# Two sequences' slots for the first routed pairs, three for the last twelve

## The chip, the cores and the metric

One core of a Trainium2 chip runs the kernel, a forward pass of two layers in float32. The metric is device time in microseconds for one execution. TensorE is called PE, VectorE DVE, ScalarE ACT, GpSimd POOL and SyncE SP, as the profile does.

## The reference

Four sequences of 512 tokens with 256 features go through two layers. The first layer is an attention inside each token, then two experts of which each token takes one. The second is a selective scan along the sequence with eight states, then a mixture of 64 routed experts (six per token) and one shared expert. What matters here is the mixture: each expert takes only the first 64 tokens that choose it, in the order of the tokens of all four sequences, and the rest is dropped.

```python
x = x + _L0_attn_ref(_layernorm(x), ...)     # B, L, E, H = (4, 512, 256, 16)
x = x + _L0_ffn_ref(_layernorm(x), ...)      # 2 experts, FF = 1024, one per token
x = x + _L1_attn_ref(_layernorm(x), ...)     # scan, d_state = 8:
    _, h = associative_scan(combine, (dA, dBu), axis=1)
    y = jnp.einsum('bldn,bln->bld', h, C_ssm) + x * D_param
x = x + _L1_ffn_ref(_layernorm(x), ...)      # H, F, E, TOP_K, CAP = 256, 176, 64, 6, 64:
    topk_w, topk_idx = jax.lax.top_k(softmax(x @ gate_w.T), TOP_K)
    pos = jnp.arange(T * TOP_K) - starts[eid_s]        # place within the expert
    valid = pos < CAP
    g = silu(einsum('ech,ehf->ecf', buf, w_gate)); u = einsum('ech,ehf->ecf', buf, w_up)
    d = jnp.einsum('ecf,efh->ech', g * u, w_down)
    y = jnp.einsum('tkh,tk->th', out_exp.reshape(T, TOP_K, H), topk_w)
    y = y + silu(x @ sh_gate.T) * (x @ sh_up.T) @ sh_down.T
```

## The kernel before

Steps are Python closures that record instructions; `_together` deals several lists of them into one order by their lengths, and a scheduler then sets the order on each engine. At run time every engine works its own queue strictly in that order and waits on semaphores.

The first layer's experts are taken in tiles of 128 tokens (`hidden`, `turned`, `down`), two halves to a tile, and run beside the scans of the first three sequences. `down` ends with a scatter of `yo` into `back` by POOL, and `join` loads `back` on SP and adds it to the sequence's `x`.

The second layer of a sequence is `scan_inputs` (layernorm, projections, softplus), eight times `state`, `scan_out`, `scores`, `choose` and `ranked`. In `state`, PE spreads one row of B and one of C over the partitions (`bc`), DVE multiplies, scans twice and multiplies again, and ACT computes the decays. The products are added up by an accumulating DMA of POOL for the first three sequences and on DVE for the fourth. `scores` also stores the normalized rows with their 64 scores in DRAM (`xrow`). `choose` marks each token's six experts, `ranked` takes the first 64 tokens of each expert by eight rounds of a maximum of eight and a replacement, and `slots` merges such lists of several sequences into the 64 places of each expert, and into the row numbers that gathers and scatters use.

The routed experts go in 32 pairs (`routed`). For a pair, POOL gathers 128 rows (`gather`, tile `xg`), PE turns them (`tokens`, `mtp`) and multiplies by gate and up (`up`, `mgu`), PE turns the result (`turn`, `mth`), multiplies by the down weights (`down`, `mpo`), ACT and DVE scale the halves (`mdw`), and POOL scatters them, adding, into one of two tables `ytab`. The 1.03 MB of a pair's weights are loaded on SP (`moe_weights`), six pairs ahead: pair 0's buffer is in a pool of its own, the other five lie where the first layer's weights were.

`slots(0)` merges the lists of three sequences and comes after the third scan, so no pair starts before that. The steps of `shared` of the first two sequences come there as well. Then the 32 pairs are dealt among the fourth sequence's scan and the third's shared expert; the fourth's shared expert comes after the pairs. The tables are loaded and added to three sequences at the end. If an expert still has room after three sequences and the fourth wants it, the block behind `tc.If(any_new > 0)` computes all pairs again for the fourth sequence.

Of the kernel before, what the change touches and what calls it, by code (L numbers as in the profile page):

```python
# [16 lines left out]
P = 128  # L17
# [20 lines left out]
AHEAD = 1  # L38
AHEAD0 = 5
PART = NB - 1  # L40
TP = PART * L
TL = T - TP
# [16 lines left out]
def two_layer_kernel(  # L59
# [30 lines left out]
    moew = ctx.enter_context(tc.tile_pool(name="moew", bufs=AHEAD))  # L90
# [5 lines left out]
    xrow = dram.tile([TP, XR], F32, name="xrow")  # L96
    xlast = dram.tile([TL, XR], F32, name="xlast")
# [87 lines left out]
    lists = keep.tile([64, 4, CAP], F32, name="lists")  # L185
    later_lists = keep.tile([64, 3, CAP], F32, name="later_lists")
    masks = keep.tile([P, NJ, 2, E1], F32, name="masks")
    raws = [keep.tile([P, E1 // 2], F32, name=f"raw{i}") for i in range(2)]
    slot_tok = [keep.tile([P, E1 // 2], U32, name=f"slot_tok{i}") for i in range(2)]
    slot_row = [keep.tile([P, E1 // 2], U32, name=f"slot_row{i}") for i in range(2)]  # L190

    def moe_weights(g, pool):

        wgu = pool.tile([P, 2, 2, 2, F1], F32, tag="wgu", name=f"wgu{g}")
        wd = pool.tile([FH, 2, 2, D], F32, tag="wd", name=f"wd{g}")
        pair = slice(2 * g, 2 * g + 2)
        nc.sync.dma_start(wgu[:, :, 0, :, :], wg1[pair].rearrange("e (p c) f -> p e c f", c=2))
        nc.sync.dma_start(wgu[:, :, 1, :, :], wu1[pair].rearrange("e (p c) f -> p e c f", c=2))
        nc.sync.dma_start(wd, wd1[pair].rearrange("e (p c) h -> p e c h", c=2))
        return wgu, wd  # L200

    with ExitStack() as st:
# [26 lines left out]
        def later_loads():  # L229
# [14 lines left out]

            return [moe_weights(g, moew) for g in range(AHEAD)]

# [258 lines left out]
        def gated_experts(tiles, joins):  # L505
# [4 lines left out]
            def step(n):  # L510
# [17 lines left out]
                if 0 <= n - 2 < len(halves):  # L528
                    (*_, down, i), f = halves[n - 2]
                    down(i, f)  # L530
                    if (n - 1) % (2 * NT0) == 0:
                        joins[(n - 1) // (2 * NT0) - 1]()
# [11 lines left out]
        def second_layer(b):  # L544
# [46 lines left out]
            def state(n):  # L591
# [8 lines left out]
                nc.vector.tensor_tensor(w, s["du"], bc[0], ALU.mult)  # L600
# [56 lines left out]

            def keep_rows():
                to = xrow[b * L : (b + 1) * L, :] if b < PART else xlast[:, :]
                nc.sync.dma_start(to.rearrange("(j p) c -> p j c", p=P), s["xr"][:, :, 0:XR])  # L660

            def choose():
# [18 lines left out]
                else:  # L681
                    for h in range(2):
                        part = rest[:, 2 * h : 2 * h + 2, 0:E1]
                        nc.vector.tensor_scalar(mask[:, :, h, :], part, -3.0, None, ALU.is_equal)

# [17 lines left out]
            def shared(i):  # L703
                f0, fn = SH_CHUNKS[i]
                early = b < PART - 1
# [10 lines left out]
                if early:  # L716

                    h = w0.tile([P, L], F32, tag="h", name=f"sh{b}_{i}", bufs=3)
                else:
                    h = wk.tile([P, L], F32, tag=("run", "left", "xd")[i], name=f"sh{b}_{i}")  # L720
# [3 lines left out]
            def shared_down():  # L724

                bank = {"tag": "o"} if b == PART - 1 else {"tag": "bc", "bufs": 2}
# [10 lines left out]
            counting = ([keep_rows] if b == PART else []) + [lambda: ranked(lists[:, 2:4, :] if b == 2 else later_lists[:, 1:3, :])]  # L737
            if b == 1:
                steps += [lambda: ranked(lists[:, 0:2, :])]
            elif b == 2:  # L740
                steps += counting
            return scan_inputs, states, steps, counting, [lambda i=i: shared(i) for i in range(3)] + [shared_down]

        def slots(i):

            n = 3 if i else 4
            all_lists = later_lists if i else lists
            v = wk.tile([P, L], F32, tag="run", name=f"merge{i}")[0:64, 0 : n * CAP]
            nc.vector.tensor_copy(v, all_lists.rearrange("e n s -> e (n s)"))
            best = sm.tile([64, CAP], F32, tag="slots", name=f"slots{i}", bufs=1)  # L750
            greatest(best, v)
            if i == 0:
                nc.vector.tensor_copy(later_lists[:, 0, :], best)
                chain["slots"] = best
            tpt = ps.tile([CAP, E1], F32, tag="tp", bufs=2, name=f"tpt{i}")
            nc.tensor.transpose(tpt, best, ident[0:64, 0:64])
            by_pair = tpt.rearrange("s (g e) -> s e g", e=2)

            raw = raws[i]
            for e in range(2):  # L760
                nc.vector.tensor_scalar(raw[64 * e : 64 * e + 64, :], by_pair[:, e, :], -1.0, float(T), ALU.mult, ALU.add)
            to = sm.tile([P, E1 // 2], F32, tag="to", name=f"to{i}")
            if i == 0:
                nc.vector.tensor_scalar_min(slot_tok[i], raw, float(TP - 1))

                full = sm.tile([P, E1 // 2], F32, tag="full", name=f"full{i}")
                nc.vector.tensor_scalar(full, raw, float(TP), None, ALU.is_lt)
                nc.vector.tensor_scalar(to, raw, odd[:, i : i + 1], spare[:, i : i + 1], ALU.add, ALU.subtract)
            else:
                nc.vector.tensor_scalar(to, raw, float(TP), 0.0, ALU.subtract, ALU.max)  # L770
                nc.vector.tensor_scalar_min(slot_tok[i], to, float(TL - 1))

                full = sm.tile([P, E1 // 2], F32, tag="full", name=f"full{i}")
                nc.vector.tensor_scalar(full, raw, float(T), None, ALU.is_lt)
                nc.vector.scalar_tensor_tensor(full, raws[0], float(TP), full, ALU.is_ge, ALU.mult)
                nc.vector.tensor_scalar(to, to, odd[:, i : i + 1], spare[:, i : i + 1], ALU.add, ALU.subtract)
            nc.vector.tensor_tensor(to, to, full, ALU.mult)
            nc.vector.tensor_scalar(slot_row[i], to, spare[:, i : i + 1], None, ALU.add)  # L778
# [3 lines left out]
        def routed(i, table, sums):  # L782
# [3 lines left out]

            def gather(g):
                xg = s["xg", g] = mo.tile([P, XR], F32, tag="xg", name=f"xg{i}_{g}", bufs=6)
# [3 lines left out]
                    in_=table[:, :],  # L792
                    in_offset=bass.IndirectOffsetOnAxis(ap=slot_tok[i][:, g : g + 1], axis=0),
                    bounds_check=(TL if i else TP) - 1,
# [26 lines left out]
            def turn(g):  # L821
# [5 lines left out]
                nc.vector.tensor_copy(ht, th)  # L827

            def down(g):
# [9 lines left out]
                for e in range(2):  # L839
# [8 lines left out]
                    out_offset=bass.IndirectOffsetOnAxis(ap=slot_row[i][:, g : g + 1], axis=0),  # L848
# [18 lines left out]
        ahead = {(0, g): w for g, w in enumerate(later_loads())}  # L867
# [14 lines left out]
        shared, routing = [], []  # L882
        inputs, *_ = layers[0]
        inputs()
        for b in range(PART):
            _, states, steps, _, next_shared = layers[b]

# [4 lines left out]
            part = experts[(b + 1) * halves + LEAD : (b + 2) * halves + LEAD]  # L892
            _together((scan, len(scan)), (part, len(part)), (zero, len(zero)))
            shared, routing, zero = shared + next_shared, steps[1:], []
            if b < PART - 1:
                inputs, *_ = layers[b + 1]
                inputs()
            steps[0]()
        for step in routing:
            step()  # L900
        slots(0)

        for step in shared[0 : -len(next_shared)]:
            step()
        first.close()
        mw0 = ctx.enter_context(tc.tile_pool(name="mw0", bufs=AHEAD0, side="right", reuse_waits="tile"))
        mo = ctx.enter_context(tc.tile_pool(name="mo", bufs=2, side="right", reuse_waits="tile"))
        pools = [moew] * AHEAD + [mw0] * AHEAD0
        for g in range(AHEAD, len(pools)):
            ahead[0, g] = moe_weights(g, mw0)  # L910
        inputs, *_ = layers[PART]
        inputs()
# [3 lines left out]
        gather, tokens, up, turn, down = routed(0, xrow, lambda g: ytabs[g % 2 if g < TURNS else 0])  # L916
# [17 lines left out]
        def end(g):  # L934
            down(g)
            if g + len(pools) < NG:
                ahead[0, g + len(pools)] = moe_weights(g + len(pools), pools[g % len(pools)])
# [23 lines left out]
        _, states, steps, counting, last_shared = layers[PART]  # L961
        scan = states + steps

        def more():

            pc = ps.tile([E1, 1], F32, tag="tp", bufs=2, name="pc")
            mask = chain["mask"]
            for j in range(NJ):
                nc.tensor.matmul(pc, mask[:, j // 2, j % 2, :], ones, start=(j == 0), stop=(j == NJ - 1))
            new = sm.tile([E1, 1], F32, tag="new", name="new")  # L970
            nc.vector.scalar_tensor_tensor(
                new, chain["slots"][:, CAP - 1 : CAP], 0.0, pc, ALU.is_equal, ALU.mult
            )
            pn = ps.tile([1, 1], F32, tag="tp", bufs=2, name="pn")
# [5 lines left out]
        rest = []  # L980
        for n, step in enumerate(scan + [more]):
            rest += [step] + (next_shared[n // 2 : n // 2 + 1] if n % 2 else [])
        _together((rest, len(rest)), (pairs, len(pairs)))
# [14 lines left out]
        with tc.If(any_new > 0):  # L998
            for i in range((2 * TL + P) // P):
                nc.sync.dma_start(ylast[i * P : (i + 1) * P, :], zero_row)  # L1000
            for step in counting:
                step()
            slots(1)
            gather, tokens, up, turn, down = routed(1, xlast, lambda g: ylast)
            for g in range(NG):
                ahead[1, g] = moe_weights(g, pools[g % len(pools)])
                for step in (gather, tokens, up, turn, down):
                    step(g)
            for k in range(2):
                y = wk.tile([P, NJ, D], F32, tag="w", name=f"yl{k}", bufs=3)  # L1010
# [50 lines left out]
```

## Time and profile before

| what | value |
|---|---|
| median of 3 runs | 637.59 us (633.24 to 639.61) |
| profiled execution, its own time | 637.62 us |
| its span, first to last instruction | 635.8 us |
| mean granted PE clock | 0.915 |
| PE, DVE, ACT, POOL busy | 522.7, 435.5, 338.0, 157.7 us |
| first multiply of the third sequence's scan | 326.29 us |
| first gather of a pair | 421.80 us |
| first multiply of the fourth sequence's scan | 443.54 us |
| last `mdw` of the last pair ends | 603.10 us |

Times inside the run are counted from the start of the span. A line of a timeline gives start, duration, engine, source line, operation, tiles, and in brackets the idle time of the engine before it with what ended it. Instructions are pipelined, so a duration can be a little longer than the distance to the next start. Where instructions of one kind follow each other, the line has their number behind an x and the duration of the row as a whole.

### The profile page before, as it was taken

How to read it: one execution, taken by the hardware profiler on the slowest of the kernel's cores; microseconds unless marked ns; L12 is line 12 of the kernel's file. 1: busy time of each engine (PE TensorE's matmuls, PEld its weight loads, DVE VectorE, ACT ScalarE, POOL GpSimd, SP SyncE). 2: the span in 40 equal slices, each digit the busy share in tenths (PEclk: the TensorE clock that was granted, in tenths of full speed). 3: DMA queues.
4: the chain of work that ended last, by engine and by line, in shares of the span. 5: the costliest groups of instructions: out<-in, count | busy, mean ns of one | idle time of the engine just before them, and what ended most of it. 6: DMA issues, size and time to landing. Idle time of an engine off the chain costs nothing.

```text
span 635.8 us, 7427 instructions
## 1 busy us (share of the span) xinstructions
PE 522.7 (82%) x2197; PEld 304.7 (48%) x2197; DVE 435.5 (69%) x907; ACT 338.0 (53%) x501; POOL 157.7 (25%) x136
## 2 busy tenths in 40 slices
PE   3289999999989999998997618957887889789970
PEld 2276767666445556565563305523433444445440
DVE  4848384624396887989889997855978873244463
ACT  2116464734887749896696404129787953115200
POOL 6011213030012110221001200030457456444410
PEclk9769999999999999999999958966788989899985
DMA  8982011012337740354104530964799999996397
GB/s 249 367 210 85 26 42 35 26 50 83 100 97 183 205 121 1 100 112 96 25 2 115 101 73 1 259 169 125 173 270 238 260 277 269 261 256 148 57 287 241
DMA packets 67438, 92.09 MB, mean 145 GB/s; under 512 B 7741, under 2 KB 56383, under 8 KB 67392
## 3 DMA queue, kind: packets, MB, share of 16 engines
q1 hardware_dynamic: 55024, 67.47, 35.0%
q0 software_dynamic: 10464, 23.09, 17.8%
q10 hardware_dynamic: 1904, 0.98, 0.5%
q8 instruction: 21, 0.34, 0.2%
q14 instruction: 25, 0.20, 0.1%
HBM read 60.68 MB, written 21.92 MB: 130 GB/s over the span
## 4 chain that ended last, share of the span: by engine, by line
PE 53%; DVE 22%; DMA 12%; ACT 7%; issue 5%; SPq 0%; POOL 0%; DVEq 0%; POOLq 0%; ACTq 0%
PE pg L453 8%; PE pu L453 7%; PE po L473 7%; DVE w L603 5%; DMA xg<-xrow,slot_tok 5%; PE mgu L813 5%; PE mpo L836 4%; PE pq L302 3%; DVE w L600 3%; DMA y<-ytab 3%; DMA ytab<-mdw,slot_row 3%; PE th L463 2%; PE pso L730 2%; PE psu L710 2%; PE px L554 1%
## 5 line engine op out<-in xcount | busy, mean ns | idle before, releaser
L846 POOL DMA_INDIRECT ytab<-mdw,slot_row x32 | 57.3, 1792 | 86.5 <-DVE mdw L845 71.1
L473 PE MATMUL po<-wd,ht 128*128 x320 | 77.3, 380 | 0.6 <-issue 0.6
L453 PE MATMUL pg<-wg,xet 128*128 x160 | 76.9, 595 | 0.0
L603 DVE TENSOR_TENSOR_SCAN w<-da,w 128x512 f32<-128x512 f32 x64 | 75.9, 1210 | 0.7
L453 PE MATMUL pu<-wu,xet 128*128 x160 | 76.0, 593 | 0.0
L473 PEld LDWEIGHTS po<-wd,ht 128*128 128x128 f32 x320 | 57.3, 190 | 14.4 <-issue 8.6
L813 PE MATMUL mgu<-wgu,xt 128*64 128x352 f32 x256 | 61.1, 556 | 3.5 <-ACT xt L804 3.5
L486 POOL DMA_INDIRECT back<-yo,xe x18 | 21.2, 1176 | 117.7 <-ACT yo L483 116.2
L789 POOL DMA_INDIRECT xg<-xrow,slot_tok x32 | 34.8, 1088 | 61.5 <-DVE slot_row L778 52.0
L602 ACT ACTIVATE da<-delta,aneg 128x512 f32<-128x512 f32 x64 | 44.4, 717 | 9.8 <-DVE w L603 9.5
L453 PEld LDWEIGHTS pu<-wu,xet 128*128 128x128 f32 x160 | 29.6, 190 | 35.3 <-issue 33.2
L836 PE MATMUL mpo<-wd,mht 88*64 88x256 f32 x256 | 39.1, 414 | 6.5 <-DVE mdw L845 5.8
L596 PE MATMUL bc<-parts,sel 96*128 96x512 bf16 x64 | 23.9, 398 | 23.9 <-DVE w L612 12.8
L456 ACT ACT_TABLE_LOAD x28 | 35.9, 1283 | 13.3 <-PE pg L453 12.9
L600 DVE TENSOR_TENSOR w<-du,bc 128x1024 f32<-128x1024 f32 x32 | 38.6, 1207 | 5.4 <-PE bc L596 4.0
L602 ACT ACT_TABLE_LOAD x31 | 39.8, 1283 | 4.8 <-DVE w L603 4.3
L458 DVE TENSOR_TENSOR h<-sg,pu 128x512 f32<-128x512 f32 x40 | 27.1, 679 | 21.4 <-PE pu L453 12.6
L453 PEld LDWEIGHTS pg<-wg,xet 128*128 128x128 f32 x160 | 28.9, 190 | 24.5 <-issue 20.4
L618 POOL DMA_DIRECT2D acc<-w x18 | 15.9, 884 | 90.8 <-DVE w L612 62.9
L456 ACT ACTIVATE sg<-pg 128x512 f32<-128x512 f32 x40 | 23.9, 597 | 26.3 <-PE pg L453 26.0
L396 POOL DMA_INDIRECT by_expert<-xnf,at x16 | 16.7, 1045 | 84.4 <-DVE at L392 46.3
L813 PEld LDWEIGHTS mgu<-wgu,xt 128*64 128x64 f32 x256 | 24.4, 157 | 26.2 <-issue 11.7
(228 smaller groups left out, 943.8 us busy)
## 6 DMA issues: line engine op xcount, KB each, us to landing
wgu<-in_L_ffn_w_gate_dram SPq DMA_DIRECT2D x32, 352.0 KB
wgu<-in_L_ffn_w_up_dram SPq DMA_DIRECT2D x32, 352.0 KB
wd<-in_L_ffn_w_down_dram SPq DMA_DIRECT2D x32, 352.0 KB
acc<-w POOLq DMA_DIRECT2D x18, 512.0 KB
ytab<-blank SPq DMA_DIRECT2D x50, 128.0 KB
y<-ytab SPq DMA_DIRECT2D x12, 512.0 KB
by_expert<-blank SPq DMA_DIRECT2D x18, 129.0 KB
xe<-by_expert SPq DMA_DIRECT2D x18, 129.0 KB
```

Of the source, the lines that this page charges most:

```text
L453: nc.tensor.matmul(t, s["xet", i][:, c, :], rhs, start=(c == 0), stop=(c == 1))
L456: nc.scalar.activation(sg, pair[0], AF.Silu)
L458: nc.vector.tensor_tensor(h, sg, pair[1], ALU.mult)
L473: nc.tensor.matmul(po, s["ht", i, f][:, k, :], rhs, start=(f == 0 and k == 0), stop=(f == 1 and k == NF // 2 - 1),)
L596: nc.tensor.matmul(t, sel[:, k * NS + n, :], parts, start=True, stop=True)
L600: nc.vector.tensor_tensor(w, s["du"], bc[0], ALU.mult)
L602: nc.scalar.activation(da[:, c, :], s["delta"][:, c, :], AF.Exp, scale=aneg[:, c, n : n + 1])
L603: nc.vector.tensor_tensor_scan(w[:, c, :], da[:, c, :], w[:, c, :], 0.0, ALU.mult, ALU.add)
L789: nc.gpsimd.indirect_dma_start(out=xg, out_offset=None, in_=table[:, :], in_offset=bass.IndirectOffsetOnAxis(ap=slot_tok[i][:, g : g + 1], ...
L813: nc.tensor.matmul(gu[rows, :, :], xt[:, c, rows], wgu[:, e, :, c, :], start=(c == 0), stop=(c == 1))
L836: nc.tensor.matmul(po[rows, :], ht[:, c, rows], wd[:, e, c, :], start=(c == 0), stop=(c == 1))
L846: nc.gpsimd.indirect_dma_start(out=sums(g)[:, :], out_offset=bass.IndirectOffsetOnAxis(ap=slot_row[i][:, g : g + 1], axis=0), in_=dw, in_o ...
```

## The change

All rows of `xrow` lie in one table for four sequences, and rows and scores are stored separately. After `ranked` of the second sequence, `slots(0)` merges the lists of two sequences. A new function `in_order` counts which pairs have both experts full by then, and builds with four small matmuls a permutation of the experts that puts these pairs first. The permuted numbers go to SBUF as integers (`order`), and `moe_weights` reads each pair's number into a register of SP, which gives the address of its three loads. Scores are permuted in the same way (`turn_scores`, `keep_scores`) before they are stored.

The first 20 pairs (`EARLY`) use the slots of two sequences, the last 12 those of `slots(1)`, which merges three. The third sequence's scan is begun with its first three states beside the rest of the first layer's experts; its other states, the fourth sequence's `join` and `scan_inputs`, and the third sequence's `scan_out`, `scores`, `choose`, `ranked` and `slots(1)` are dealt among the pairs, together with the fourth scan and the shared experts of three sequences. The separate buffer of pair 0 is gone: weights are held for five pairs. The copy `ht` moves from DVE to ACT. The block behind `tc.If` now also covers the third sequence, and is entered too if an early pair had room after two sequences.

```diff
-AHEAD = 1
-AHEAD0 = 5
+EARLY = 20
+AHEAD = 5
+BEGUN = 3
...
     def moe_weights(g, pool):
...
-        pair = slice(2 * g, 2 * g + 2)
+        with tc.issue_after(chain["weights"].ins) if chain.get("weights") else ExitStack():
+            e = nc.sync.value_load(order[0:1, 2 * g : 2 * g + 1], min_val=0, max_val=E1 - 2)
+        pair = bass.ds(e, 2)
...
+            def turn_scores():
+                tp = ps.tile([E1, L], F32, tag="tp", bufs=2, name=f"tps{b}")
+                for j in range(NJ):
+                    nc.tensor.transpose(tp[:, bass.ts(j, P)], s["xr"][:, j, D:XR], ident)
+                nc.scalar.copy(scores_t[:, b % 2, :], tp)
+
+            def keep_scores():
+                pp = ps.tile([P, NJ, E1], F32, tag="tp", bufs=2, name=f"psc{b}")
+                for j in range(NJ):
+                    nc.tensor.matmul(pp[:, j, :], scores_t[:, b % 2, bass.ts(j, P)], perm, start=True, stop=True)
+                sc = sm.tile([P, NJ, E1], F32, tag="ordered", name=f"ordered{b}", bufs=1)
+                nc.scalar.copy(sc, pp)
+                nc.sync.dma_start(rows_to[:, :, D:XR], sc)
...
         def slots(i):
-            n = 3 if i else 4
-            all_lists = later_lists if i else lists
+            n = (2, 3, 5)[i]
...
             if i == 0:
-                nc.vector.tensor_copy(later_lists[:, 0, :], best)
-                chain["slots"] = best
+                chain["hold"] = in_order(best)
             tpt = ps.tile([CAP, E1], F32, tag="tp", bufs=2, name=f"tpt{i}")
-            nc.tensor.transpose(tpt, best, ident[0:64, 0:64])
+            nc.tensor.matmul(tpt, best, perm, start=True, stop=True)
...
+        def in_order(best):
+            full = sm.tile([64, 1], F32, tag="o_full", name="o_full", bufs=1)
+            nc.vector.tensor_scalar(full, best[:, CAP - 1 : CAP], 0.0, None, ALU.is_gt)
+            both = ps.tile([64, 1], F32, tag="tp", bufs=2, name="o_both")
+            nc.tensor.matmul(both, same, full, start=True, stop=True)
+            nc.vector.tensor_scalar(whole[:, 0:1], both, 2.0, 0.5, ALU.is_ge, ALU.mult)
...
+            nc.vector.tensor_scalar(perm, rank[0:64, 0:E1], at[:, 3:4], None, ALU.is_equal)
+            pn = ps.tile([1, E1], F32, tag="tp", bufs=2, name="o_numbers")
+            nc.tensor.matmul(pn, number, perm, start=True, stop=True)
+            chain["weights"] = chain["fetch"]
+            return nc.vector.tensor_copy(order, pn)
...
-                nc.vector.tensor_copy(ht, th)
+                nc.scalar.copy(ht, th)
...
-        for step in routing:
-            step()
-        slots(0)
-        for step in shared[0 : -len(next_shared)]:
-            step()
+        scores, choose, ranked = routing
+        scan = [scores, choose, states[0], ranked, lambda: slots(0)] + scored[0:2] + states[1:BEGUN]
+        _together((scan, len(scan)), (part, len(part)))
         first.close()
...
-        _, states, steps, counting, last_shared = layers[PART]
-        scan = states + steps
+        inputs, last_states, last_steps, late, last_shared = layers[PART]
+        rest = states[BEGUN:] + [joins[PART], inputs] + steps + [lambda: slots(1), scored[2]]
+        first_shared = len(rest) - 6
+        rest += last_states + last_steps
...
-        rest = []
-        for n, step in enumerate(scan + [more]):
-            rest += [step] + (next_shared[n // 2 : n // 2 + 1] if n % 2 else [])
-        _together((rest, len(rest)), (pairs, len(pairs)))
+        dealt = rest[0:first_shared]
+        others = rest[first_shared:] + [more]
+        for n, step in enumerate(others):
+            dealt += [step] + shared[n * len(shared) // len(others) : (n + 1) * len(shared) // len(others)]
+        _together((dealt, len(dealt)), (pairs, len(pairs)))
```

## The prediction

> **What bounds the kernel now.** I read the page's header first, then busy time by stage (windows), the waits and the chain, and last the timelines of PE, DVE and GpSimd, for the price of one piece.
>
> ```profile
> span 635.8 us, 7427 instructions
> ...
> ## 4 chain that ended last, share of the span: by engine, by line
> PE 53%; DVE 22%; DMA 12%; ACT 7%; issue 5%; SPq 0%; POOL 0%; DVEq 0%; POOLq 0%; ACTq 0%
> ```
>
> The whole does not tell which engine to relieve, as the stages differ. Busy time by window (columns: PE, weight loads, DVE, ACT, GpSimd, then granted clock, DMA share, GB/s):
>
> ```profile
> 328.00:421.00 93.00, 59.27 (x210) 33.72 (x209) 85.88 (x201) 31.61 (x44) 8.97 (x9) 0.84 0.45 114
> 421.00:512.00 91.00, 75.18 (x326) 34.16 (x326) 66.94 (x92) 72.39 (x101) 42.92 (x29) 0.81 0.77 205
> 512.00:603.00 91.00, 80.68 (x449) 43.83 (x446) 39.54 (x105) 31.36 (x66) 46.67 (x35) 0.96 0.83 209
> 603.00:636.00 33.00, 13.29 (x39) 7.77 (x37) 17.09 (x19) 1.19 (x2) 2.56 (x1) 0.75 0.83 264
> ...
> 512.00:573.00 61.00, 51.79 (x280) 28.10 (x276) 25.01 (x57) 17.18 (x39) 33.15 (x26) 0.94 0.99 266
> ```
>
> From 328 (third scan) to 421 DVE is full and PE has a third of its time free. Then all 32 pairs run, with DMA full from 512 to 573 and PE close behind. The chance the change sees is the first row: GpSimd waits for the slots until 421.8.
>
> ```profile
> POOL xg L789 <- DVE slot_row L778: 52.0, 1, 52.0
> ...
> 421.80 1.10 POOL L789 DMA_INDIRECT xg<-xrow,slot_tok  x1 [51.99 <-DVE slot_row L778]
> ...
> 282.64 3.85 DMA back<-back
> ```
>
> The last line, from the chain, is the load that `join` waits for. PE's prices, where it runs dense:
>
> ```profile
> 406.40 6.02 PE L730 MATMUL pso<-shd,sh 128*128 128x256 f32 x24
> ...
> 531.34 1.09 PE L836 MATMUL mpo<-wd,mht 88*64 88x256 f32 x8
> 532.26 1.40 PE L813 MATMUL mgu<-wgu,xt 128*64 128x352 f32 x8
> 533.59 0.46 PE L825 MATMUL mth<-ident,mh 128*88 128x128 f32 x2
> 533.89 0.45 PE L802 MATMUL mtp<-ident,xg 128*128 128x128 f32 x2
> 534.27 1.09 PE L836 MATMUL mpo<-wd,mht 88*64 88x256 f32 x8
> ...
> 603.80 1.88 PE L710 MATMUL psu<-xnt_r,shu 128*128 128x512 f32 x4
> ```
>
> A pair costs 534.27 - 531.34 = 2.93 us; a chunk of the shared expert, two such groups of four, 3.5; its down step 6.0: 16.5 for one sequence. On DVE I use distances between starts, since neighbours overlap a little:
>
> ```profile
> 344.01 1.21 DVE L600 TENSOR_TENSOR w<-du,bc 128x1024 f32<-128x1024 f32 x1
> ...
> 356.37 0.68 DVE L540 MAX8 best<-rank 128x8 f32<-128x512 f32 x1
> ...
> 458.68 1.21 DVE L620 TENSOR_TENSOR acc<-acc,w 128x1024 f32<-128x1024 f32 x1
> ```
>
> One such pass is 1.13 us (344.01 to 345.14), so a state is 1.13 + 2.25 (two scans) + 1.13 = 4.5, and 5.65 with the fourth sequence's accumulate.
>
> **The change, step by step, against the profiled run (span 635.8, time 637.62, 1.8 around it; the median is 637.59, practically the same).** Up to 328.0 the queues hold the same work; the new constants are small memsets, comparisons and selects early on, at 0 (to +2 if they delay the first layer).
>
> *The order known.* DVE finishes state 0, scores and choose at 336.4 (8.4 us of the same instructions). The ranking's transposes now stand on PE behind the first layer's last `pu`; with ACT's table loads the last `h` comes out near 340.9. Ranking 512 wide: 8 rounds less one replace, 1.43 each alone: 11.0 with the first multiply's rest. Copies 0.6. The merge is now 128 wide, which the trace lacks: between 0.40 (two steps of 0.20, as on 64 columns, L675) and 0.97 (256 wide) a round; by the slope from 512 to 256 I take 0.74, 5.7 in all. `in_order`: eleven tiny DVE steps at 0.15 (the row of `new`, L971) and four trips over PE at some 0.65: 4.2. Order at 362.5.
>
> *Weights.* They can't be fetched before it (before, they lay in SBUF at 413). On SP stand first a register load, and two stores of scores, the second waiting for the first because `ordered` has one buffer (3 to 5 us). The register loads show in no row: between 0 and 1.2 us (a pair's three issues at 0.4); SP is idle more than half of each pair's time, so nothing, or 38 us spread over 32 pairs at worst without cover. Streaming begins at about 371, the first `mgu` at 380 instead of 428: a head start of 48 us.
>
> *Third scan's rest.* Seven states at 4.5, the slots' small steps 1.5: 362.5 + 33 = 395.5, with three `mh` 397.
>
> *The join of the fourth sequence.* This was hidden: `back` landed long before 376. Now its load stands on SP behind the weights of pair 7, which wait until pair 2 has left its buffer (near 399); on DVE the addition stands behind `mh` of pair 6. Lower bound: 399 + 3.85 (the row above) = 403. Upper bound: everything issued since 371 passes first: 7.9 MB of weights at 266 GB/s (the full window) 30 us, eight gathers of 0.16 MB 5, six accumulating stores of 512 KB 18 (in 328 to 385 they took 31.8% of the engines' time), and the load 2: 426. The table loads at the end speak for a queue: their additions end one by one, 2 us apart. I take 418. By the Trainium skill, DMA: Bandwidth & Descriptors (Queues, rings and completion order), each DMA engine consumes a ring's descriptors in order; strictly applied that gives 426 and a time 8 us above mine, the bare row one 15 us below. No row of before has a small load behind such a stream.
>
> *Inputs of the fourth sequence.* Addition, statistics and normalization 6 us, then, as from 305.07 (first `tp_s`) to 326.29 (first `w`), 21 to 23: 28. Scan at 446.
>
> *The block to the second slots.* On PE the `bc` matmuls of states 3 to 7 stand one after the other, with no pair between, and then the transpose of the second slots: PE can't pass until DVE has done all of it. DVE's queue there: 8 states 36.1, state 0's skip 1.3, six accumulates 6.8, closing halves 1.2, ranking 256 wide 7.3, merge 192 wide 5.6 (between 0.74 and 0.97 a round, less the overlap), scores and choose 3.6, five `mh` and four `mdw` 3.1, three `sh` 1.8, slots 0.6: 67.3. Slots at 514 (499 and 522 by the join's bounds). By then pairs 0 to 12 are up and 0 to 10 down, and only the first shared expert's chunks are done. Before, by 512, there were 16 and 14, two whole shared experts and two chunks of a third: the head start is spent, since PE had some 30 us of this block idle.
>
> *The rest.* PE must do 19 pairs (55.7), two more downs (2.6), the first shared down (6.0), two shared experts (33), scores of the fourth sequence (5.0), counts and permuted scores (1.8): 104.1. DMA has 17.3 MB of weights, 16 gathers 2.6, 21 scatters 2.8: 22.7 MB at 266 = 85 us, hidden by PE unless it bunches. So the last pair ends at 618, and not at 603.1. Behind it lies the same tail (scatter, six loads, adds, store): 635.8 - 603.1 = 32.7, span 650.8.
>
> *At nothing:* `ht` on ACT (32 x 0.42 moves from DVE, where only 13 copies stand in the full block; ACT has slack before 446 and after 514, up to +5 if not); the score transposes (0.4 on PE, 0.9 on ACT each); five weight buffers for six, covered because PE and not DMA paces the end. Closing additions keep their place.
>
> **Sum:** 418 + 28 + 67.3 + 104.1 + 32.7 + 1.8 = 652. It is 14 us above the run before.
>
> **Rivals.** *Early join*: the load overtakes the stream; 403 in place of 418: 637, and 632 if the block has its small waits overlapped too. For it speaks the 3.85 us row, against it a DMA share of 0.99 under such a stream. *Head start kept*: PE gets on with pairs and shared work during the fourth scan, as it does from 421 to 512 now (75 of 91 us); then the end of the pairs moves up by the 48 us, less the 16 us (91 - 75) that PE lacks for it even now: 606. This holds only if DVE reaches the slots by about 485; its 150 us of work after 328 with no wait whatever would end at 478. *DMA bunches*: shared steps and transfers don't overlap evenly and the last 85 us of DMA and 104 of PE cover each other only partly; 10 to 15 us more: 665. *The reserve branch runs*, because a pair given early has room left: 32 pairs one after the other at over 10 us each, near 1000. Counting the reference's choices, 27 of 32 pairs are full after two sequences, 20 are needed, and all 64 experts after three, so it should not.
>
> **How the numbers follow.** Forecast (644 to 662) 0.58, early join (627 to 642) 0.22, head start kept 0.07, bunching 0.11, reserve 0.02. About 1% is what a measurement of this kernel can tell from no change, its runs lying 1% apart: below 631 faster, above 644 slower. Faster: 0.07 and 0.08 of the early join, 0.15. Same: 0.14 of it and 0.06 of the forecast's low end, 0.20. Slower: 0.52 + 0.11 + 0.02 = 0.65. The range 630 to 670 takes in the join's bounds (637 to 660), bunching's middle and most of the early join.
>
> **What would show it.** Right: gathers from about 370; the fourth sequence's `join` at 410 to 426 after a DMA wait; PE mostly idle in the last 35 us ahead of the second slots; those slots at 505 to 522; then PE at nine tenths or more with its clock at 1.0 until about 618, and a tail of 33. Wrong: slots before 490, PE busy beside the fourth scan, or pairs ending before 600.

## The result, and the profile after

The changed kernel takes 686.45 us (median of four runs, 678.66 to 690.82); the kernel before, on the same chip, 638.60. The ratio is 1.0715, with a 95% interval of 1.0581 to 1.0848: slower by some 7%. The forecast was 652 with a range to 670, so the sign was right and the size was not: 48 us were lost and 14 were forecast. The profiled execution, whose span of 689.0 us is taken apart below, is the slowest of the four, 4 us above their median; up to the fourth sequence's join its times recur within 0.3 us in a fast execution of the second experiment (third scan's closing additions at 428.3 for 428.1, join at 441.7 for 441.9).

The header of the page of the changed kernel, and its chain by engine:

```profile
span 689.0 us, 7864 instructions
...
## 4 chain that ended last, share of the span: by engine, by line
PE 18%; DVE 10%; DMA 8%; issue 3%; ACT 1%; SPq 1%; DVEq 0%; ACTq 0%; POOLq 0%
```

This chain could be followed back to 408.7 us only, and so its shares add up to 41% of the span: the 18% of PE can't be set beside the 53% of before. The windows cover the whole. Busy time by window (start and end, length, then PE, weight loads, DVE, ACT, GpSimd with their counts, granted clock, DMA share, GB/s):

```profile
364.00:430.00 66.00, 32.61 (x122) 17.83 (x120) 36.51 (x43) 20.16 (x34) 16.62 (x15) 0.66 0.80 199
430.00:471.00 41.00, 34.94 (x127) 15.73 (x125) 20.58 (x49) 22.64 (x38) 14.36 (x10) 0.73 0.63 163
471.00:502.00 31.00, 28.97 (x133) 14.19 (x133) 26.89 (x58) 23.79 (x40) 13.51 (x8) 1.00 0.66 175
502.00:539.00 37.00, 5.82 (x13) 1.11 (x11) 36.85 (x66) 7.85 (x10) 2.64 (x2) 0.56 0.18 46
539.00:600.00 61.00, 58.31 (x309) 33.95 (x310) 17.69 (x44) 20.15 (x51) 26.56 (x21) 0.96 0.81 216
600.00:656.00 56.00, 51.00 (x265) 28.26 (x262) 20.09 (x62) 20.75 (x44) 20.75 (x15) 0.94 0.66 154
```

Two rows are bad. From 502 to 539 PE does 5.8 us of work in 37 while DVE is full: this loss the prediction had named. From 364 to 430 neither PE (33 of 66) nor DVE (37 of 66) is busy, though DVE should have been through the third scan in 33 us. What it waits for stands in the list of waits (engine, tile and line that waited, what released it: us in total, times, longest):

```profile
DVE acc L662 <- DMA acc<-w: 14.3, 1, 14.3
DVE w L636 <- DMA acc<-w: 11.4, 4, 5.2
```

These are the accumulating stores (`acc<-w`) of the third scan, which the prediction had only counted as traffic. Their times from issue to landing in the changed kernel:

```profile
DMA to landing us min/median/max: 6.7/8.9/9.8
```

GpSimd's timeline shows them in the changed kernel, with the first gather of a pair above:

```profile
381.66 1.08 POOL L874 DMA_INDIRECT xg<-xrow,slot_tok  x1 [0.30 <-issue]
...
388.24 1.01 POOL L654 DMA_DIRECT2D acc<-w  x1
398.55 0.92 POOL L654 DMA_DIRECT2D acc<-w  x1 [6.97 <-DMA acc<-w]
408.74 0.88 POOL L654 DMA_DIRECT2D acc<-w  x1 [9.27 <-issue]
419.12 0.86 POOL L654 DMA_DIRECT2D acc<-w  x1 [9.50 <-issue]
```

and the same stores in the kernel before:

```profile
345.18 0.89 POOL L618 DMA_DIRECT2D acc<-w  x1 [2.63 <-DMA acc<-w]
351.00 0.88 POOL L618 DMA_DIRECT2D acc<-w  x1 [4.93 <-DVE w L612]
356.09 0.86 POOL L618 DMA_DIRECT2D acc<-w  x1 [4.21 <-DVE rank L695]
```

These three came 5 to 6 us apart, the last two at the pace of DVE's work; now they come every 10. All stores add into the same `acc`, so none is issued before the one ahead of it has landed (`<-DMA acc<-w`). The tile `w` has three buffers, and a state can't begin its product before the store of three states ago has read its buffer. The chain of the changed kernel (start, us, what) shows how far that reaches:

```profile
408.74 0.88 DMA acc<-w
409.62 9.48 issue
...
419.12 8.87 DMA acc<-w
...
428.08 0.69 DVE acc L662
...
441.60 0.34 DVE mh L904
441.94 1.14 DVE x L534
```

The last store takes until 428, the closing additions follow, and with them the products `mh` of the pairs, which stand behind them in DVE's queue; the fourth sequence's addition (L534) comes behind `mh` of the seventh pair. PE's prices are the ones used (1.41 for `mgu`, 1.09 for `mpo`), except after it has stood still:

```profile
506.85 0.61 PE L630 MATMUL bc<-parts,sel 96*128 96x512 bf16 x1 [3.99 <-DVE w L636]
...
518.63 0.58 PE L630 MATMUL bc<-parts,sel 96*128 96x512 bf16 x1 [3.74 <-DVE w L648]
...
538.75 0.47 PE L805 MATMUL tpt<-perm,slots 64*64 64x64 f32 x2 [5.35 <-DVE slots L574]
...
542.24 2.21 PE L898 MATMUL mgu<-wgu,xt 128*64 128x352 f32 x8
...
599.65 1.41 PE L898 MATMUL mgu<-wgu,xt 128*64 128x352 f32 x8 [1.15 <-DVE mdw L930]
...
601.62 1.09 PE L921 MATMUL mpo<-wd,mht 88*64 88x256 f32 x8
606.17 2.62 PE L898 MATMUL mgu<-wgu,xt 128*64 128x352 f32 x8 [3.46 <-DMA wgu<-in_L_ffn_w_up_dram]
```

The first lines show the block ahead of the second slots: each spreading matmul (`bc`) waits for DVE, and the slots' transpose (`tpt`) stands behind them.

### The profile page after: what moved, and what is told of

Same layout as the page of the kernel before. It is cut to its first block, busy times and chain, and to the rows that moved or that the text cites. A ratio compares the mean times of both kernels' runs of the same rounds, so it can differ in the third digit from the quotient of the medians.

```text
span 689.0 us, 7864 instructions
## 1 busy us (share of the span) xinstructions
PE 541.7 (79%) x2252; PEld 315.7 (46%) x2252; DVE 431.5 (63%) x925; ACT 330.7 (48%) x523; POOL 156.3 (23%) x140
## 5 line engine op out<-in xcount | busy, mean ns | idle before, releaser
L931 POOL DMA_INDIRECT ytab<-mdw,slot_row x32 | 50.6, 1580 | 152.2 <-DVE mdw L930 144.1
L630 PE MATMUL bc<-parts,sel 96*128 96x512 bf16 x64 | 26.1, 431 | 47.3 <-DVE w L648 24.0
L898 PE MATMUL mgu<-wgu,xt 128*64 128x352 f32 x256 | 55.1, 536 | 6.0 <-DMA wgu<-in_L_ffn_w_up_dram 4.5
L921 PE MATMUL mpo<-wd,mht 88*64 88x256 f32 x256 | 48.7, 417 | 0.9 <-DVE mdw L930 0.9
L636 DVE TENSOR_TENSOR w<-du,bc 128x1024 f32<-128x1024 f32 x32 | 38.8, 1214 | 15.8 <-DMA acc<-w 11.4
L490 ACT ACT_TABLE_LOAD x29 | 37.2, 1283 | 14.2 <-PE pg L487 13.9
L487 PEld LDWEIGHTS pg<-wg,xet 128*128 128x128 f32 x160 | 28.8, 191 | 27.9 <-issue 20.5
L874 POOL DMA_INDIRECT xg<-xrow,slot_tok x32 | 38.9, 1215 | 9.8 <-issue 5.8
L492 DVE TENSOR_TENSOR h<-sg,pu 128x512 f32<-128x512 f32 x40 | 27.3, 682 | 21.0 <-PE pu L487 12.4
L930 DVE TENSOR_SCALAR mdw<-mpo,xg 64x256 f32<-64x256 f32 x32 | 15.7, 490 | 30.8 <-ACT mdw L928 27.6
L902 ACT ACTIVATE msg<-mgu 128x176 f32<-128x176 f32 x32 | 10.2, 318 | 51.1 <-PE mgu L898 51.0
```

The source lines that it names most:

```text
L487: nc.tensor.matmul(t, s["xet", i][:, c, :], rhs, start=(c == 0), stop=(c == 1))
L490: nc.scalar.activation(sg, pair[0], AF.Silu)
L492: nc.vector.tensor_tensor(h, sg, pair[1], ALU.mult)
L630: nc.tensor.matmul(t, sel[:, k * NS + n, :], parts, start=True, stop=True)
L874: nc.gpsimd.indirect_dma_start(out=xg, out_offset=None, in_=xrow[0:n, :], in_offset=bass.IndirectOffsetOnAxis(ap=slot_tok[k][:, g : g + 1] ...
L898: nc.tensor.matmul(gu[rows, :, :], xt[:, c, rows], wgu[:, e, :, c, :], start=(c == 0), stop=(c == 1))
```

## The experiments

Theory A: the third scan's accumulating stores are late, and through DVE the join and the whole fourth scan. Theory B: PE is held ahead of the second slots by the spreading matmuls (`bc`) of the fourth scan's states. Rival C: transfers pace the end, and what is won ahead of the slots is lost behind them. Where nothing else is said an edit is made to the changed kernel. "Slots" with a time means the slots' transpose on PE, and "the last scaling" the end of the last `mdw`.

**One cause at a time.** The third scan adds up on DVE:

```diff
-                    elif b < PART:
+                    elif b < PART - 1:
                         nc.gpsimd.dma_start(s["acc"], w, accum_op=ALU.add)
```

> The third sequence's scan adds up its products on DVE instead of by six accumulating stores of POOL; nothing else changes. Theory A (these stores land late beside the weight stream and the gathers, 8.9 us at the median between 364 and 430, and DVE and with it the pairs' own multiplications wait for them): DVE pays 6 x 1.13 = 6.8 us more but loses waits of about 26 us, so the third scan's closing additions start near 405 to 412 instead of 428, the addition of the fourth join near 418 to 428 instead of 441.9, and everything behind moves up by 14 to 24 us: 660 to 672 us. Rival C (the weights themselves set the pace there, so that pair 6, which stands ahead of the join on DVE, is no earlier): the closing additions move up, but the join stays at 437 or later and the time within 5 us of 686. Rival of sign: the 6.8 us are not hidden and the waits were slack: 690 or more.

Measured: 666.95 us, 19.5 less. DVE's timeline:

```profile
415.50 1.29 DVE L662 TENSOR_TENSOR acc<-acc,w 128x512 f32<-128x512 f32 x2
...
426.79 1.23 DVE L534 TENSOR_TENSOR x<-x,back 128x1024 f32<-128x1024 f32 x1 [4.94 <-DMA back<-back]
```

The closing additions start 12.6 us earlier (3.5 behind the expected end) and the join 15.1, though the first load of weights is issued 4.4 us later in this execution (377.5 for 373.1). The second slots come at 519.9 and not at 538.8, 18.8 earlier, and the last scaling ends 20.5 us earlier: what is won ahead of the slots isn't lost behind them, so C falls for this edit. Only now does the join wait for its own load, as the prediction had thought: issued on SP at 412.9, landed at 426.8.

**The second slots first.** Nothing is added; DVE ranks and merges ahead of the fourth scan's states 2 to 7:

```diff
+                hold = chain["hold"] if b == PART - 1 and n else chain["second"] if b == PART and n >= 2 else None
-                with tc.issue_after(chain["hold"].ins) if b == PART - 1 and n else ExitStack():
+                with tc.issue_after(hold.ins) if hold else ExitStack():
                     nc.vector.tensor_tensor(w, s["du"], bc[0], ALU.mult)
...
-            greatest(best, v)
+            chain["second"] = greatest(best, v)
```

(`greatest` now returns its last maximum.)

> On DVE, states 2 to 7 of the fourth scan are put behind the last maximum of the second slots; before, this ranking and merge alternated with them. No instruction is added or removed. Theory B (PE is held for some 35 us by the matmuls that spread B and C for states 3 to 7, which stand ahead of the second slots' transpose): five to six states of 5.65 us leave the block, the transpose comes near 505 to 512 instead of 538.75, PE gets on with the pairs while DVE does the states beside them, and the end of the pairs moves up by 22 to 32 us: 654 to 665 us. Rival C (weights and gathers pace the pairs after the slots anyway, PE has only exchanged one wait for another): the transpose is as early, but the pairs take 140 us or more behind it and the time stays above 678. Rival D (the states, now among the pairs, make PE wait for DVE at each spread, as they did, only later): 670 to 680.

Measured: 660.58 us, 25.9 less. From PE's timeline and the windows:

```profile
510.30 0.44 PE L807 MATMUL tpt<-perm,slots 64*64 64x64 f32 x2 [8.14 <-DVE slots L574]
```

```profile
510.00:540.00 30.00, 28.75 (x139) 15.94 (x139) 26.98 (x40) 19.45 (x33) 10.24 (x7) 0.91 0.57 141
```

The transpose comes 28.5 us earlier, and in the 30 us behind it PE (28.8) and DVE (27.0) are both busy: the states that had blocked PE now run beside pairs. The last scaling ends 28.6 us earlier (629.94 for 658.57). B holds; C and D, which said 670 or more, don't.

**Both**, the two diffs above together.

> Both edits: sums of the third scan on DVE, and the second slots ahead of states 2 to 7 of the fourth scan. If A and B are two separate losses on one chain, the gains add up: 14 to 24 and 22 to 32 us give 632 to 650, about the time of the kernel before. If transfers pace the rest (C), the second gain is met by a full DMA: 26 MB of weights still to come at 266 GB/s need about 98 us from the slots on, and the time is 655 or more.

Measured: 641.22 us, 45.2 less than the changed kernel; the single gains are 19.5 + 25.9 = 45.4. The two gains add up, as those of two losses that lie one behind the other on one chain. Against the kernel before the ratio is 1.0104 (1.0054 to 1.0154).

**What makes the stores late.** The first attempt left loads out:

```diff
-        ahead = {(0, g): moe_weights(g, mw0) for g in range(AHEAD)}
+        ahead = {(0, 0): moe_weights(0, mw0)}
+        ahead.update({(0, g): ahead[0, 0] for g in range(1, AHEAD)})
```

> Pairs 1 to 4 compute with the weights of pair 0, so that four of the first five pairs' loads (4.3 MB) are left out; results of these pairs are those of other weights. The accumulating stores stay as they are. Theory A (the stores of the third scan are slowed by the stream of weights): with a stream of one pair instead of five ahead of 400 they land in 5 us as before the change, the third scan's closing additions start by 410 instead of 428, and the time falls by 10 to 20 us. Rival E (the stores are late because they stand behind gathers on POOL's own queue, or because of the states' own order): they still follow each other at 9 to 10 us, the closing additions start at 420 or later, and the time falls by less than 8 us.

Measured: 663.74 us (a single execution, as in the next three and in the run with eight loads left out), but the stores were issued from 372 to 417, nearly as in the changed kernel (373 to 419), and the closing additions began at 421.9: the loads of later pairs had moved up into the free buffers. So the edit didn't take the stream away, and can't tell the theories apart. The gain goes with the join: its load was issued at 393.4 instead of 436.1, and its addition came at 422.5 instead of 441.9. The next one shares pair 0's weights among pairs 0 to 11, with the same flaw:

```diff
+        ahead.update({(0, g): ahead[0, 0] for g in range(1, 12)})
...
-            if g + AHEAD < NG:
+            if 12 <= g + AHEAD < NG:
                 ahead[0, g + AHEAD] = moe_weights(g + AHEAD, mw0)
```

> Pairs 0 to 11 compute with the weights of pair 0, so that between 373 and some 430 only one pair's weights (1.06 MB) are loaded; results of these pairs are those of other weights. In the run that left out four loads the later pairs' loads moved up into their place (6.9 MB came between 364 and 430 against 8.6), so it did not take the stream away; this one does. The six accumulating stores and the gathers are as in the changed kernel. Theory A1 (the stream of weights slows the stores): they follow each other at 5 to 6 us, as before the change (345.18, 351.00, 356.09, 361.96), the closing additions start by 410 instead of 428, time 645 to 665. Theory A2 (what slows them is the gathers and scatters, which go through the same software queue of POOL): stores 8 to 10 us apart, closing additions at 418 or later, and the time falls only by what pairs gain from not waiting for weights, to 660 to 680.

Measured: 669.45 us, closing additions at 421.4; again five pairs' loads were issued by 399. Its figures fit A2 as expected, but the premise of A1 was not met. The gathers were then held instead, and the third scan recorded ahead of the pairs:

```diff
-            for g in range(3):
-                gather(g)
+            with tc.issue_after(chain["acc"].ins):
+                gather(0)
+            for g in range(1, 3):
+                gather(g)
```

> The first gather stands on POOL behind the last accumulating store of the third scan, so that the stores run with the weight stream beside them (five pairs, 5.3 MB, some 20 us at 266 GB/s) but without gathers and scatters. No instruction is added. A1 (the stream slows the stores): the first three or four stores are still 7 to 10 us apart. A2 (gathers on the same queue slow them): all are 5 to 6 us apart, the closing additions start near 405. The time is no test here, since the pairs begin late: between 670 and 700.

Measured: 676.32 us. GpSimd's last stores:

```profile
391.31 0.85 POOL L654 DMA_DIRECT2D acc<-w  x1 [8.35 <-DMA acc<-w]
401.50 0.86 POOL L654 DMA_DIRECT2D acc<-w  x1 [9.33 <-issue]
410.68 0.85 POOL L654 DMA_DIRECT2D acc<-w  x1 [8.32 <-issue]
```

and DVE's closing additions behind the last one:

```profile
415.32 1.31 DVE L662 TENSOR_TENSOR acc<-acc,w 128x512 f32<-128x512 f32 x2 [8.32 <-DMA acc<-w]
```

Without a single gather they are 9 to 10 us apart: gathers are not needed for the delay. The DMA share stayed at 0.7 to 1.1 until 408 in this run; the last store, issued behind that, let DVE go on after 4.6 us, at 415.3. A busy DVE isn't what makes them late either: in the kernel before it worked without a gap from 345 to 356 (11.0 of 11 us busy), where the stores came every 5 to 6 us. Last, with pairs 0 to 11 sharing weights as before, the stream was really held:

```diff
+        if g == 12 and "closed" in chain:
+            tc.add_manual_dep(late.ins, chain.pop("closed").ins.name, DATA, reason="after the third scan")
```

(`late` is the first load of a pair's weights, `closed` the third scan's last closing addition.)

> Pairs 0 to 11 compute with the weights of pair 0 (their results are those of other weights), and the load of pair 12 waits for the third scan's closing additions. In the two earlier runs that shared weights the later pairs' loads simply moved up into the free buffers (five pairs were loaded between 373 and 399 all the same), so the stream was never gone; here only 1.06 MB of weights come before the third scan ends. Gathers, scatters and the six accumulating stores remain. A1 (the stream of weights makes the stores late): from the third on they follow each other at 5 to 6.5 us instead of 9 to 10, and the closing additions start at 396 to 408 instead of 428. A2 (gathers and scatters on the stores' own queue do it): still 8 to 10 us, closing additions at 418 or later. The run with the gathers held, in which the stores still were 8 to 10 us apart, speaks for A1. Time 650 to 670, no test in itself.

Measured: 666.4 us, closing additions at 413.5, and the stores:

```profile
391.68 1.02 POOL L656 DMA_DIRECT2D acc<-w  x1
...
398.23 0.92 POOL L656 DMA_DIRECT2D acc<-w  x1 [3.33 <-DMA acc<-w]
403.39 0.88 POOL L656 DMA_DIRECT2D acc<-w  x1 [4.24 <-DVE w L641]
408.46 0.86 POOL L656 DMA_DIRECT2D acc<-w  x1 [4.19 <-DVE w L641]
```

6.6, 5.2 and 5.1 us apart, the last two paced by DVE again. The run with the same shared weights and no hold issued its last three stores at 398.6, 408.7 and 416.5, and in neither run, nor in the changed kernel, does GpSimd issue a gather or scatter between the last three: A1 is shown for these. The store of 383.4, beside the end of pair 0's weights, the join's load and five gathers, still took 8.2 before the next was issued. So it seems that whatever fills the transfer engines (share 1.00 from 388 to 396) delays a store; gathers alone were not tried. That store, and a start 2.9 us later than in the changed kernel (first load at 376.0 for 373.1), go with additions 5 us later than expected.

**The stretch behind the slots.** It took 119.8 us where the prediction had 104.1.

```diff
-                ahead[0, g + AHEAD] = moe_weights(g + AHEAD, mw0)
+                h = g + AHEAD
+                ahead[0, h] = ahead[0, h - 1] if h > 16 and h % 2 else moe_weights(h, mw0)
```

> From pair 17 on each odd pair computes with the weights of the pair before it: eight loads of 1.06 MB are left out of the stretch behind the second slots, 8.4 MB or 32 us at 266 GB/s (the results of these pairs are those of other weights). Everything ahead of the slots is as in the changed kernel: slots near 539. Theory U (PE's own work paces that stretch, which took 119 us from the slots to the last scaling where the prediction had 104): the stretch stays at 114 to 119 us, time 680 to 688. Theory V (it is paced by weights that come late; the chain there has 24% of its time in waits for them): 104 to 110 us, time 670 to 678.

Measured: 687.04 us, not faster. First the wait for weights in the changed kernel from 539 to 656, which is gone in this run; then this run's windows:

```profile
PE mgu L898 <- DMA wgu<-in_L_ffn_w_up_dram: 4.5, 2, 3.5
```

```profile
539.00:600.00 61.00, 60.74 (x300) 35.79 (x302) 16.19 (x41) 19.55 (x50) 26.37 (x20) 0.89 0.68 176
600.00:656.00 56.00, 54.20 (x289) 30.29 (x285) 23.15 (x67) 22.13 (x47) 22.01 (x16) 1.00 0.37 72
```

With DMA at 0.68 and 0.37 PE no longer waits for weights and is busy 60.7 of 61, and the stretch still takes 115.3 us (537.74 to 653.01), 4.5 less: U holds, PE's own work paces it, at a granted clock of 0.89 in the first half.

**Can the order be kept?** In the kernel with both edits PE waits 10.5 us for the fourth sequence's layernorm, because its join comes 11.6 us behind the closing additions. Its PE timeline has the wait:

```profile
425.09 2.10 PE L299 MATMUL tp_s<-ident,xns 128*128 128x128 f32 x8 [10.45 <-DVE xns L292]
```

Two moves forward, to that kernel, the first with the layernorm (made a step of its own, `norm`):

```diff
-        rest = states[BEGUN:] + [joins[PART], inputs] + steps + ...
+        left3 = states[BEGUN:]
+        rest = [joins[PART]] + left3[:-2] + [chain["norm", PART]] + left3[-2:] + [inputs] + steps + ...
```

> To the kernel with both edits (sums on DVE, second slots first; 641.2 us): the fourth sequence's join is recorded ahead of the third scan's five last states, and its layernorm ahead of the last two, instead of after the third scan. The load then stands on SP behind five pairs' weights and not behind six or seven. In the kernel with both edits the addition came at 420.9, 11.6 us behind the closing additions, and the fourth scan at 447.7. Theory P (PE now paces everything behind the slots: 113 of 118 us busy from 492 to 610; what can be won is PE's idle time ahead of them, 18 us from 364 to 420, 8 from 420 to 448, 10 from 448 to 492): the fourth scan starts 12 to 20 us earlier, PE's idle time shrinks by some 8 to 10, and the time is 629 to 635. Rival Q (the chain over DVE to the second slots paces the end one for one, as in the two edits before): 621 to 628. Rival R (DVE is full in the third scan, the join only takes its place there): 638 or more.

Measured: 652.35 us, 11 more and not 6 to 20 less. The number is in R's range, but DVE was not full (47.4 of 56 us from 364 to 420). PE's timeline shows why nothing was won:

```profile
414.17 2.09 PE L299 MATMUL tp_s<-ident,xns 128*128 128x128 f32 x8 [8.94 <-DVE xns L292]
...
425.90 1.88 PE L596 MATMUL px<-xnt_s,wx 128*64 128x512 f32 x4
```

The transposes still made PE wait, and the projection that needs them was dealt behind pairs, nearly 12 us later. The fourth scan began at 447.7, as without the move. The slots came 4.6 us later (496.4 for 491.9); why the whole lost 11 us is not settled beyond that. With the first shared expert dealt beside the third scan as well:

```diff
-        dealt = rest[0:first_shared]
+        dealt = []
+        for n, step in enumerate(rest[0:first_shared]):
+            dealt += [step] + shared[n : n + 1] * (n < 4)
+        shared = shared[4:]
```

> As the one before, and the first sequence's shared expert (16.5 us of PE, some 4 of DVE) is dealt beside the third scan's last states, the second's from there on. Theory P: it fills PE's 18 us of idle time between 364 and 420; the time falls by 6 to 12 us against the one before, to 618 to 628. Rival Q: its 4 us on DVE come into the chain to the second slots, and the time rises by 2 to 5 us.

Measured: 645.64 us, 6.7 less than the run before it, though the slots came 11 us later (507.1 for 496.4): from 364 to 448 PE did 14 us more work (72.4 for 58.3 busy). The difference is P's, the level of 618 to 628 is not reached. Moving the join alone:

```diff
-        rest = states[BEGUN:] + [joins[PART], inputs] + steps + ...
+        rest = [joins[PART]] + states[BEGUN:] + [inputs] + steps + ...
```

> To the kernel with both edits (641.2 us): only the fourth sequence's join is recorded ahead of the third scan's last five states, its layernorm stays behind the scan. In the run that moved both (652.4 us), the addition came at 407 but the transposes of the layernorm stood on PE ahead of three pairs' work and the projection behind it, so that the fourth scan started at 447.7 as without the edit, and PE had 9 us of idle time. With the join alone, the addition comes near 406, the layernorm follows the closing additions at once, PE's wait of 10.5 us ahead of it shrinks to nothing, the fourth scan starts at 434 to 440 and the slots come at 478 to 486 instead of 491.9. Theory P (the end follows PE's idle time ahead of the slots): 630 to 636 us. If the move does nothing on balance: 638 to 644.

Measured: 632.79 us, against the kernel before 0.9916 (0.9877 to 0.9954). DVE's timeline:

```profile
407.37 1.20 DVE L534 TENSOR_TENSOR x<-x,back 128x1024 f32<-128x1024 f32 x1
...
413.57 0.67 DVE L664 TENSOR_TENSOR acc<-acc,w 128x512 f32<-128x512 f32 x1
```

The addition no longer waits for its load, the fourth scan starts at 440.0 and the slots come at 479.5. The slots are 12.4 us earlier than with both edits, the last scaling 8.8: no longer one for one, as P said. This version is the fastest, 0.8% below the kernel before. With the shared expert moved too, by the diff above:

> As the one before, and the first sequence's shared expert (16.5 us of PE) is dealt beside the third scan's last states. In the pair of runs with the layernorm moved this made 652.4 into 645.6 us, although the slots came 11 us later. P: 6 us less than the run before it here too, 624 to 631. If PE has no idle time left to fill there: as the run before, or 2 to 5 us more, for its 4 us on DVE.

Measured: 634.91 us, within the spread of the run before it and not the 6 us less that P had; against the kernel before it is 0.994 (0.9899 to 0.9981). The slots came 15 us later (494.6), and what PE gained by the earlier work it lost again: busy 6.1 us more from 364 to 420, 5.7 less from 448 to 603.

## Why the prediction was right in sign and wrong in size

| step | predicted | profile | difference in the step itself |
|---|---|---|---|
| order known | 362.5 | 363.8 | +1 |
| first `mgu` | 380 | 389.9 | +9, not on the path |
| third scan's rest ends | 397 | 429 | +31 |
| join of the fourth sequence | 418 | 441.9 | +24 on the path |
| inputs of the fourth sequence | 28 | 29.3 | +1 |
| block to the second slots | 67.3 | 67.6 | 0 |
| the rest, to the last scaling | 104.1 | 119.8 | +16 |
| tail | 32.7 | 30.4 | -2 |

From 652 the differences from the join on (24 + 1 + 0 + 16 - 2) lead to 691, the profiled execution.

*The step that failed first is the third scan's rest.* "Seven states at 4.5" priced DVE's work alone. The stores behind these states were entered in the bounds of the join as 18 us of traffic, never as something that DVE waits for, although the kernel before gives their spacing and `w` has three buffers. The stream that the change starts at 373 about doubles their time, DVE stands still for 25.7 us (14.3 + 11.4), and the pairs with it. With the sums on DVE 19.5 of the 34 us by which 652 was short are gone. By the Trainium skill, DMA: Bandwidth & Descriptors (Queues, rings and completion order), a DMA engine with work on several queues takes turns between them packet by packet. That agrees with these runs: about 5 us for a store without a stream (4.6 for the last one with the gathers held; 5.2 between 340.0 and 345.2 in the kernel before), 9 to 10 with one, the stores on GpSimd's queue and the weights on SP's. The turns themselves no run here shows. The prediction applied that section to the join's load alone.

*The join's own price was sound, its place on the path was not.* That the addition stands behind `mh` of pair 6 was in the prediction, but not how late that would be. Its load took 13.9 us to land behind the weights in the run with the sums on DVE (412.9 to 426.8), and 14 with both edits, against 3.85 in the kernel before, so "a queue" was the right reading. But in the changed kernel the load was issued at 436.1 only and the addition stood behind `mh` of pair 6: the queue that mattered was DVE's. With the stores gone the load was issued at 412.9, and at 406.9 with both edits, still not near 399, and the join came 8.8 and 2.9 us behind 418. The 426 for a strict order on one ring was worked out with gathers and stores in front, which GpSimd issues and not SP. The rival of an early join fell with it.

*The inputs and the block* were right to a microsecond, and the cause given for the block (the `bc` matmuls of states 3 to 7 ahead of the transpose) is shown by the run with the second slots first. What the prediction left out is that this block is a choice of order: taken apart, it is worth 26 us. As this loss was named and is there, the sign was not luck.

*The rest* was mis-sized. The count of work was right (152 `mgu` matmuls are 19 pairs; 160 `mpo` until 656 are 20 downs, and one more follows), and the reading that PE paces it too; the run with eight loads less gives 115.3 us for it without waits for weights. The prices were those of a clock of 1.0, and PE came out of a block of 37 us with 5.8 us of work. In the run with eight loads less its clock was 0.89 over 61 us, by an estimate (0.11 x 61) 6.7 of the 11 us by which 115.3 exceeds 104.1; in the changed kernel it was 0.96 and 0.94, 5.8 us by the same estimate. Another 4.5 us of the changed kernel's stretch are waits for weights, so the rival of bunched DMA is a small part of it. The last 4 to 5 us are not settled.

*Rivals.* "Head start kept" asked for the slots by 485; the version that meets this (479.5) takes 632.8 and not 606, as PE then has its own work left. The reserve branch did not run: from the last scaling to the end it is 30.4 us, less than the 32.7 before. The price of nothing for the register loads, and for `ht` on ACT, was not tried alone.

## What to carry to other kernels

Before work with a stream of loads is moved beside other work, look for the transfers that the other work waits for, and price these at what they take beside the stream (here about twice their time), not only the engines' work. Count for every in-order engine what stands behind such a wait: here a late store held DVE, DVE held the pairs' products, these held PE and the next sequence's join. And where two chains alternate on one engine while a third waits for one of them, put that one first.

## What the runs showed of the hardware

A 512 KB accumulating store between two tiles in SBUF took about 5 us with little else moving (4.6 and 5.2) and 9 to 10 beside a stream of weights at a DMA share near 1.0, with gathers or without. After a wait a group of eight `mgu` matmuls took 2.62 us instead of 1.41, at 606 after only 3.5 us of idle time, and 2.21 at 542 after the long block; the granted clock was 0.50 from 606 to 609 and from 537.8 to 542.2. A dense price holds only in a dense stretch. Loads left out of the front of a queue bring the later ones forward: two experiments that meant to thin a stream left it nearly as it was until 404.
